# xn^T kn of batches 1 to 7 as seven block products, with its block sums on GpSimd

## The chip, the cores and the metric

The kernel runs on one core of a Trainium2 chip. A core has five engines, each with an instruction queue of its own that it works through in order: TensorE (PE; its weight loads are listed as PEld), VectorE (DVE), ScalarE (ACT), GpSimd (POOL) and SyncE (SP), which here only issues transfers. They meet through semaphores. Matmul results land in PSUM, everything else lives in SBUF. The metric is the time on the device in microseconds (us); less is better.

## The reference, cut to what matters

The input `x` has 8 batches of 1024 rows of 256 channels, in 32-bit floats. The result is `x` plus a linear attention plus a two-layer network, both fed with the normalised `x`.

```python
xn = (x - mean(x)) / sqrt(var(x) + 1e-5)             # per row
q, k, v = split(xn @ qkv_w + qkv_b)                  # 16 heads of 16 channels
q, k = q / max(|q|, 1e-12), k / max(|k|, 1e-12)      # per row and head
kv  = einsum('bhnd,bhne->bhde', k, v)
out = einsum('bhnd,bhde->bhne', q, kv)
ffn = relu(xn @ W1 + b1) @ W2 + b2
return x + out @ proj_w + proj_b + ffn
```

The kernel never forms `v`. It takes G = xn^T kn (256 x 256, kn being the scaled k), multiplies by the weights of v to get the 16 x 16 blocks of `kv`, and folds these with `proj_w` into one 256 x 256 matrix M, so that the attention's output is q M.

## The kernel before

**Tiling.** A batch is 8 tiles of 128 rows. `xn` and `qk` hold rows on partitions; `xnT` and `qT` hold channels on partitions, and come from 32x32 transposes on VectorE (`turn`) whose squares the SP queue moves into place. Batches go in a loop over `b` (line 822) with these steps on PE: `hidden(b)` (the first layer, with small steps put between its products), `project_by_sums(b + 1)` (q and k of the next batch; `project(1)` for batch 1), the first half of `second(b)` (the second layer and q M, up to the `yield` on line 762), `mix_g(b + 1)`, and the second half of `second(b)`.

**Block products.** `hidden`, `project_by_sums` and `second` use a scheme for a product of two 2 x 2 block matrices that takes seven block products for eight. It needs sums of blocks of both factors: four of the left (s1 to s4, `sums_of_a`, line 188) and four of the right (t1 to t4, `sums_of_b`, line 181), some written over a block that is no longer needed (s3, t3). Sums of data are made on GpSimd. Partial results pass from bank to bank as u1, u2, u3 on VectorE.

**The mix.** `mix_g` (line 497) is a plain product: for each of two halves of xn's channels, 8 row tiles, 128 columns of xn as weights against the 256 columns of kn, summed in one bank of the pool `ps_mix`; one ScalarE copy brings the bank to `gT`. It is used by `mix_kv` (line 510) in the next `hidden`. `kn` is there once GpSimd has scaled k in place (line 466, two instructions, at the end of the projection).

**Order.** The program is written in the order wanted (`manual_schedule`), so an engine's queue has its instructions in the order of the Python calls. Within `second`, the banks are a, c_, d, e: products into a and c_, u2 (line 749), a product into d, u3 (line 753), then the function `between` (line 754, `norms_of_q` of the next batch: squares on ScalarE, their sums and inverse roots on VectorE), the product into e, and `join(1, 1)`: an addition of bank, bias and u3 on VectorE (line 719), a transpose on VectorE (line 710), an addition to `xq` on GpSimd (line 715). After that half come the statistics of x of batch b + 2 (`norm_stats`, line 241, `norm_scale`, line 255), the mix, the normalisation (`norm_apply` on ScalarE, line 271), the transposes `turn_x`, the second half of `second`, and `shift`, which adds 1 to the first 128 channels of xn.

**Buffers.** Pool `one` has one buffer per tag, so a tile waits for the last reader of the tile before it under the tag. Pool `psum` hands out seven banks in turn, `ps_mix` is the eighth. Tags that matter: "turn" (the squares of a transpose), "u1" and "u3" (partial results), "xn", "qk", "gT".

Of the kernel before, what the change touches and what calls it, by code (L numbers as in the profile page):

```python
# [9 lines left out]
F32 = mybir.dt.float32  # L10
AF = mybir.ActivationFunctionType
ALU = mybir.AluOpType
# [4 lines left out]
def kernel(  # L17
# [34 lines left out]
    nc = tc.nc  # L52
    P = 128
    B, N, C = x.shape
# [3 lines left out]
    NT = N // P  # L58
    HT = NT // 2
    HN = N // 2  # L60
    KC = C // P
# [10 lines left out]
    big = ctx.enter_context(tc.tile_pool(name="big", bufs=2))  # L72
    one = ctx.enter_context(tc.tile_pool(name="one", bufs=1))
    work = ctx.enter_context(tc.tile_pool(name="work", bufs=2))
    small = ctx.enter_context(tc.tile_pool(name="small", bufs=4))
    psum = ctx.enter_context(tc.tile_pool(name="psum", bufs=7, space=bass.MemoryType.PSUM))
    ps_mix = ctx.enter_context(tc.tile_pool(name="ps_mix", bufs=1, space=bass.MemoryType.PSUM))

# [11 lines left out]
    def bank(shape, name):  # L90

        return psum.tile(shape, F32, tag="bank", name=name)

    xs, xqs, xns, xnTs, xSs, hTs, qks, qTs, mixes, Ms, hSs = ({} for _ in range(11))
# [146 lines left out]
    def norm_stats(b, tiles):  # L241

        xt, n = xs[b], len(tiles)
        st = work.tile([P, NT, 6], F32, tag="st", name=f"st_{b}_{tiles[0]}")[:, :n, :]
        mv = small.tile([P, NT, 2], F32, tag="mv", name=f"mv_{b}_{tiles[0]}")[:, :n, :]
        for i, t in enumerate(tiles):
            nc.vector.bn_stats(st[:, i, :], xt[:, t, :])
        for i in range(n):
            nc.vector.bn_aggr(mv[:, i, :], st[:, i, :])
        rstd = small.tile([P, NT], F32, tag="rstd", name=f"rstd_{b}_{tiles[0]}")[:, :n]  # L250
        nc.scalar.activation(rstd, mv[:, :, 1], AF.Sqrt, bias=eps_sb)
        for i, t in enumerate(tiles):
            stats[b, t] = i, mv, rstd

    def norm_scale(b, tiles, on_act):
        i, mv, rstd = stats[b, tiles[0]]
        nc.vector.reciprocal(rstd, rstd)
        if on_act:
            nmr = small.tile([P, NT], F32, tag="nmr", name=f"nmr_{b}_{i}")[:, : len(tiles)]
            nc.vector.scalar_tensor_tensor(nmr, mv[:, :, 0], -1.0, rstd, ALU.mult, ALU.mult)  # L260
            for t in tiles:
                stats[b, t] += (nmr,)
# [87 lines left out]
    def invert(ss):  # L350

        nc.vector.tensor_scalar_max(ss, ss, L2_EPS * L2_EPS)
        nc.scalar.activation(ss, ss, AF.Sqrt)
        nc.vector.reciprocal(ss, ss)
# [19 lines left out]
    def squares_of(b, n, g, m, ss):  # L374
        sq = work.tile([P, 2, C], F32, tag="yt", name=f"sq_{b}_{n}_{g}_{m}")
        nc.scalar.activation(sq, part_of_qk(b, n, g, m), AF.Square)  # L376
        return lambda: nc.vector.tensor_reduce(
            ss[:, n * HT + 2 * g : n * HT + 2 * g + 2, :],
            sq.rearrange("p w (g d) -> p w g d", d=D), AX.X, ALU.add,
        )  # L380
# [69 lines left out]
    def norms_of_q(b):  # L450
        ss = small.tile([P, NT, H], F32, tag="ssq", name=f"ssq_{b}", bufs=1)
        late = []
        for n in range(2):
            for g in range(2):
                late.append(squares_of(b, n, g, 0, ss))
                if len(late) == 2:
                    late.pop(0)()
        late.pop(0)()
        invert(ss)
        for h in range(2):  # L460
            norms_of[b, h, 0] = ss[:, ts(h, HT), :]
# [9 lines left out]
    def scale_q(b, h):  # L471
        scale(nc.gpsimd if b == 0 else nc.vector, b, h, 0)

    def turn_q(b):

        if b not in qTs:
            qTs[b] = one.tile([P, KC, NP, P, 2], F32, tag="qT", name=f"qT_{b}")
            turns["q", b] = turn(qTs[b], qks[b], f"q_{b}")
        next(turns["q", b])
# [12 lines left out]
    def shift(b):  # L492

        part = xns[b][:, :, 0:P]
        nc.scalar.activation(part, part, AF.Identity, bias=ones)

    def mix_g(b):
        qk, xn = qks[b], xns[b]
        gp = ps_mix.tile([P, KC, C], F32, tag="mix", name=f"gp_{b}")
        for f in range(KC):  # L500
            for t in range(NT):
                nc.tensor.matmul(  # L502
                    gp[:, f, :], xn[:, t, ts(f, P)], qk[:, t, C : 2 * C],
                    start=(t == 0), stop=(t == NT - 1),
                )
        gT = one.tile([P, KC, C], F32, tag="gT", name=f"gT_{b}")
        nc.scalar.copy(gT, gp)
        mixes[b] = gT

    def mix_kv(b):  # L510
        gT = mixes.pop(b)
        kvp = ps_mix.tile([P, KC, P], F32, tag="mix", name=f"kvp_{b}")
        for c in range(KC):
            cols = slice(2 * C + c * P, 2 * C + (c + 1) * P)
            for f in range(KC):
                nc.tensor.matmul(  # L516
                    kvp[:, c, :], wqkv_sb[:, f, cols], gT[:, f, ts(c, P)],
                    start=(f == 0), stop=(f == KC - 1),
                )
        kvm = one.tile([P, KC, P], F32, tag="Mt", name=f"kvm_{b}")  # L520
        for c in range(KC):
            nc.vector.tensor_tensor(
                kvm[:, c, :].rearrange("p (g d) -> p g d", d=D),
                kvp[:, c, :].rearrange("p (g d) -> p g d", d=D),
                blk.unsqueeze(2).to_broadcast([P, G, D]), ALU.mult,
            )
        mixes[b] = kvm
# [126 lines left out]

    def later_steps(b):
        return {
            1: [lambda: mix_kv(b)],
            2: [lambda: scale_q(b, 0)],
            3: [lambda: scale_q(b, 1)],
            4: [lambda: mix_m(b)],  # L660
            5: [lambda: turn_q(b)],
            6: [lambda: turn_q(b)],
            7: [lambda: turn_q(b)],
            8: [lambda: turn_q(b)],

            11: [lambda: sums_of_q(b)],
        }
# [12 lines left out]
                skip_group_check=True,  # L680
            )

    def second(b, between=lambda: None):

        xq, hT, hS, qT, (M, Mt) = xqs[b], hTs[b], hSs[b], qTs[b], Ms[b]
        a11, a12, s3, a22 = (
            [hT[:, i + k * FH, ts(n, HP), :, :] for i in range(FH)] + [qT[:, k, ts(n, HP), :, :]]
            for n in range(2) for k in range(2)
        )
        s1, s2, s4 = ([hS[:, s, i] for i in range(FH + 1)] for s in range(3))  # L690
        b11, t3, b21, b22 = (
            [w2_sb[:, i + k * FH, ts(m, HC)] for i in range(FH)] + [M[:, k, ts(m, HC)]]
            for k in range(2) for m in range(2)
        )
        t1, t2, t4 = ([w2t[:, s, i, :] for i in range(FH)] + [Mt[:, s, :]] for s in range(3))

        def tmp(name):
            pool = work if name in ("u2", "yt") else one
            return pool.tile([P, HP, P, 2], F32, tag=name, name=f"{name}_o_{b}")

        def add(dst, p, q):
            nc.vector.tensor_tensor(dst, p, q, ALU.add)
            return dst
# [37 lines left out]
        a, c_, d, e = (bank([P, HP, P, 2], f"po{s}_{b}") for s in "acde")  # L741
# [4 lines left out]
        u1 = tmp("u1")  # L746
        nc.scalar.copy(u1, a)
        product(c_, t2, s2, True, True)
        u2 = add(tmp("u2"), c_, u1)
        u3 = tmp("u3")  # L750
        for du, u in zip(ds, parts):
            product(du, t3, [r[:, u] for r in s3], True, False)
# [69 lines left out]
    for b in range(B):  # L822
        if b > 0:
            load_squares(b, (0,) if b == B - 1 else (0, 1))
            if b + 2 < B:
                load(b + 2)
        hidden(b)
        if b == 0:
            qTs[0] = one.tile([P, KC, NP, P, 2], F32, tag="qT", name="qT_0")
            turn_on_pe(qTs[0], qks[0], "q_0")  # L830
            sums_of_w2()
            sums_of_q(0)
            shift(1)
        if b + 1 == 1:
            project(1)
            out_parts = second(b)
        elif b + 1 < B:
            project_by_sums(b + 1)
            out_parts = second(b, lambda: norms_of_q(b + 1))
        else:  # L840
            out_parts = second(b)
        next(out_parts)
        if b + 1 == 1:
            sums_of_x(1, 0)
            sums_of_x(1, 1)
            sums_of_wqk()
        if b + 2 < B:
            norm_stats(b + 2, range(NT))
            norm_scale(b + 2, range(NT), True)
        if b + 1 < B:  # L850
            mix_g(b + 1)
        if b + 2 < B:
            norm_apply(b + 2, range(NT))
            for _ in range(R):
                turn_x(b + 2)
        next(out_parts)
        if b + 2 < B:
            shift(b + 2)
# [31 lines left out]
```

## Time and profile before

The time is 623.9 us, the median of three runs (623.89, 623.9 and 624.88). One execution was profiled:

| what | value |
|---|---|
| the profiled execution's time | 624.22 us |
| its span, first to last instruction | 622.1 us |
| granted TensorE clock, share of full speed | 0.997 |
| PE, mix (`gp`, line 502): 256 records, two per matmul | 56.6 us busy, 379 ns each |
| share of the chain that is the mix | 9% |
| PE start to PE start of the mix, each batch from 1 on | 6.9 us |
| GpSimd instructions | 290 |
| idle time of GpSimd before its additions to `xq` (line 715), waiting for the transpose | 181.4 us over 30 |

A profile's "busy" of a matmul counts it to its modelled end, though the next one has begun; how fast PE moves is read from starts. A line of the timeline has the start and the length in us, the engine, the line of the program, the operation, the tiles written and read, the shapes, how many instructions are merged in it, and in brackets how long the engine stood idle before it and what ended that. The chain of waits follows the work that ended last back to the start. In the row of a group, the number after the bar is the busy time, then the mean of one instruction in ns, then idle time before.

### The profile page before, as it was taken

What the parts mean: (1) busy time and instruction counts of PE and PEld (TensorE: products, weight loads), DVE (VectorE), ACT (ScalarE), POOL (GpSimd) and SP (SyncE); (2) the same over time, 40 slices, a digit from 0 to 9 for tenths busy, and PEclk for the clock granted to TensorE, in tenths of its full rate; (3) what the DMA queues carried; (4) which work ended last, traced back from release to release, by engine and by line L of the source; (5) the groups of instructions that cost most, each with busy time, mean ns of one, the idle gap of its engine ahead of it and who ended that gap; (6) DMA issues with size and microseconds to landing.
All of it is one profiled execution on the core that took longest, in us unless ns stands there. A gap on an engine that the chain in (4) does not pass through costs nothing.

```text
span 622.1 us, 6098 instructions
## 1 busy us (share of the span) xinstructions
PE 612.8 (98%) x1843; PEld 344.2 (55%) x1843; DVE 398.8 (64%) x698; ACT 209.0 (34%) x348; POOL 351.1 (56%) x290
## 2 busy tenths in 40 slices
PE   8999999999999999999999999999999999999996
PEld 5465455556644666447564484644755557545454
DVE  6776735777648766577456874667845677428823
ACT  4356304352143422343242532325224352003500
POOL 3568927399315991269902797029951399414701
PEclk9999999999999999999999999999999999999998
DMA  7734001490025700285004820058101470004202
GB/s 232 141 59 136 1 0 29 112 188 11 0 51 127 161 1 1 68 156 116 0 1 101 189 49 0 6 129 178 29 0 26 112 132 2 0 3 99 67 0 67
DMA packets 139503, 43.26 MB, mean 70 GB/s; under 512 B 135880, under 2 KB 136272, under 8 KB 139472
## 3 DMA queue, kind: packets, MB, share of 16 engines
q1 hardware_dynamic: 139472, 42.89, 31.1%
q8 instruction: 14, 0.23, 0.2%
q14 instruction: 17, 0.14, 0.1%
HBM read 19.80 MB, written 8.39 MB: 45 GB/s over the span
## 4 chain that ended last, share of the span: by engine, by line
PE 96%; DVE 2%; DMA 1%; ACT 0%; issue 0%; SPq 0%; DVEq 0%; ACTq 0%
PE poe L678 11%; PE poa L678 11%; PE pod L678 10%; PE gp L502 9%; PE pha L555 8%; PE phe L555 8%; PE phd L555 8%; PE poc L678 6%; PE pq L330 5%; PE phc L555 4%; PE pqe L398 3%; PE pqa L398 3%; PE pqd L398 3%; PE pqc L398 2%; PE kvp L516 1%; PE mp L533 1%
## 5 line engine op out<-in xcount | busy, mean ns | idle before, releaser
L715 POOL TENSOR_TENSOR xq<-xq,yt_o 128x512 f32<-128x512 f32 x30 | 37.9, 1262 | 181.4 <-DVE yt_o L710 181.4
L562 ACT ACTIVATE hT<-hT,b_sb 128x512 f32<-128x512 f32 x96 | 68.8, 722 | 63.4 <-DVE hT L567 58.8
L190 POOL TENSOR_TENSOR hS<-hT 128x512 f32<-128x512 f32 x31 | 45.8, 1478 | 56.4 <-issue 41.5
L376 ACT ACTIVATE sq<-qk 128x512 f32<-128x512 f32 x48 | 29.0, 629 | 109.3 <-DVE qk L404 59.1
L555 PE MATMUL pha<-xnT,w_sb 128*128 128x512 f32 x128 | 65.4, 592 | 0.0
L678 PE MATMUL poa<-hT,w_sb 128*128 128x512 f32 x128 | 57.5, 592 | 0.0
L502 PE MATMUL gp<-qk,xn 128*128 128x256 f32 x256 | 56.6, 379 | 0.0
L502 PEld LDWEIGHTS gp<-qk,xn 128*128 128x128 f32 x256 | 48.6, 190 | 9.6 <-issue 3.3
L567 DVE TENSOR_TENSOR hT<-phe,u 128x512 f32<-128x512 f32 x64 | 43.7, 683 | 6.6 <-PE phe L555 4.9
L710 DVE STREAM_TRANSPOSE yt_o<-y_o 128x512 f32<-128x512 f32 x30 | 33.0, 1099 | 16.2 <-ACT y_o L765 13.9
L192 POOL TENSOR_TENSOR hS<-hT,hS 128x512 f32<-128x512 f32 x31 | 39.5, 1275 | 2.4
L191 POOL TENSOR_TENSOR hS<-hS,hT 128x512 f32<-128x512 f32 x31 | 39.4, 1272 | 2.4
L194 POOL TENSOR_TENSOR hT<-hT 128x512 f32<-128x512 f32 x31 | 40.0, 1290 | 0.0
L678 PEld LDWEIGHTS poa<-hT,w_sb 128*128 128x128 f32 x128 | 24.3, 190 | 25.0 <-issue 24.2
L297 DVE STREAM_TRANSPOSE turn_x<-xn 128x512 f32<-128x512 f32 x28 | 17.7, 685 | 31.1 <-ACT xn L271 31.1
L555 PEld LDWEIGHTS pha<-xnT,w_sb 128*128 128x128 f32 x128 | 23.8, 190 | 23.4 <-issue 20.8
L567 DVE TENSOR_TENSOR u<-phc,u 128x512 f32<-128x512 f32 x32 | 21.8, 681 | 20.0 <-ACT u L581 10.6
L581 ACT COPY u<-pha 128x512 f32<-128x512 f32 x32 | 18.4, 574 | 43.9 <-PE pha L555 43.9
L562 ACT ACTIVATE hT<-pha,b_sb 128x512 f32<-128x512 f32 x32 | 21.8, 682 | 33.1 <-PE pha L555 33.1
L555 PE MATMUL phe<-xS,w1t 128*128 128x512 f32 x64 | 32.7, 592 | 0.0
L555 PE MATMUL phd<-xnT,w_sb 128*128 128x512 f32 x64 | 32.7, 592 | 0.0
L555 PE MATMUL phc<-xS,w1t 128*128 128x512 f32 x64 | 32.7, 592 | 0.0
(165 smaller groups left out, 1189.6 us busy)
## 6 DMA issues: line engine op xcount, KB each, us to landing
xq<-in_L_attn_x_dram SPq DMA_DIRECT2D x60, 128.0 KB, 3.8
out_dram<-xq SPq DMA_DIRECT2D x60, 128.0 KB, 2.9
x<-in_L_attn_x_dram SPq DMA_DIRECT2D x14, 512.0 KB, 5.8
xnT<-turn_x SPq DMA_DIRECT2D x112, 64.0 KB, 2.1
qT<-turn_q SPq DMA_DIRECT2D x112, 64.0 KB, 2.2
x<-in_L_attn_x_dram SPq DMA_DIRECT2D x4, 256.0 KB, 4.0
w_sb<-in_L_ffn_W_dram SPq DMA_DIRECT2D x2, 512.0 KB, 7.0
w_sb<-in_L_ffn_W_dram SPq DMA_DIRECT2D x8, 128.0 KB, 3.1
```

Of the source, the lines that this page charges most:

```text
L190: eng.tensor_tensor(s1, a21, a22, ALU.add)
L191: eng.tensor_tensor(s2, s1, a11, ALU.subtract)
L192: eng.tensor_tensor(s4, a12, s2, ALU.subtract)
L194: eng.tensor_tensor(a21, a11, a21, ALU.subtract)
L398: nc.tensor.matmul(dst[:, w, :], a[:, g, :, w], rhs, start=start and w == 0, stop=stop, skip_group_check=True,)
L502: nc.tensor.matmul(gp[:, f, :], xn[:, t, ts(f, P)], qk[:, t, C : 2 * C], start=(t == 0), stop=(t == NT - 1),)
L555: nc.tensor.matmul(dst, lhsT, rhs, start=start, stop=stop, skip_group_check=True)
L562: nc.scalar.activation(block(i, n, m), src, AF.Relu, bias=b1_sb[:, fc : fc + 1])
L567: nc.vector.tensor_tensor(dst, p, q, ALU.add)
L678: nc.tensor.matmul(dst, l, r, start=start and n == 0, stop=stop and n == len(lhs) - 1, skip_group_check=True,)
L710: nc.vector.transpose(yt.rearrange("p u w r c -> p u r w c"), y.rearrange("p u (s r) w -> p u r w s", r=R),)
L715: nc.gpsimd.tensor_tensor(xh, xh, yt.rearrange("p u w r c -> p (u w) r c"), ALU.add)
```

## The change

For batches 1 to 7 the mix is made by the seven-product scheme, with the two row halves of the batch as the inner blocks and the two channel halves as the outer ones; batch 0 keeps `mix_g`. Each product has 128 x 128 weights and 128 moving columns, over four row tiles. It uses the bank of `ps_mix` and three of `psum`; five additions on VectorE and two copies on ScalarE join them into `gT`. The eight block sums are all on GpSimd: s3 and s2 of batch b + 1 in `hidden(b)` (part 0; for batch 1 just before part 1), t1, s1, t2 and t3 after the projection (part 1), t4 and s4 at the place of `between` (part 2). s3 goes over a block of xn and t3 over a block of kn; s1, s4, t1 and t2 take the buffer "turn", t4 takes "u1", s2 a new one, and the partial results of the mix take "u3". The statistics of x of batch b + 2 move from behind the first half of `second` to a place between u2 and u3. Pool `small` goes from four buffers to two.

```diff
-    small = ctx.enter_context(tc.tile_pool(name="small", bufs=4))
+    small = ctx.enter_context(tc.tile_pool(name="small", bufs=2))
...
+    gsums = {}
+    def blocks_of_xn(b):
+        return [xns[b][:, ts(n, HT), ts(f, P)] for f in range(KC) for n in range(2)]
+    def blocks_of_kn(b):
+        return [
+            qks[b][:, ts(n, HT), C + f * P : C + (f + 1) * P] for n in range(2) for f in range(KC)
+        ]
+    def g_sums(b, part):
+        a11, a12, a21, a22 = blocks_of_xn(b)
+        b11, b12, b21, b22 = blocks_of_kn(b) if part else [None] * 4
+        def tile_of(tag, name):
+            return one.tile([P, HT, P], F32, tag=tag, name=f"g{name}_{b}")
+        def sub(dst, p, q, op=ALU.subtract):
+            nc.gpsimd.tensor_tensor(dst, p, q, op)
+        if part == 0:
+            s2 = tile_of("gs2", "s2")
+            sub(a21, a11, a21)
+            sub(s2, a22, a21)
+            gsums[b] = [s2]
+        elif part == 1:
+            gs = one.tile([P, 4, HT, P], F32, tag="turn", name=f"gs_{b}")
+            s1, s4, t1, t2 = (gs[:, i] for i in range(4))
+            sub(t1, b12, b11)
+            sub(s1, gsums[b][0], a11, ALU.add)
+            sub(t2, b22, t1)
+            sub(b12, b22, b12)
+            gsums[b] += [s1, s4, t1, t2]
+        else:
+            s2, s1, s4, t1, t2 = gsums[b]
+            t4 = tile_of("u1", "t4")
+            sub(t4, b21, t2)
+            sub(s4, a12, s2)
+            gsums[b] = [s1, s2, s4, t1, t2, t4]
+    def mix_g_by_sums(b):
+        a11, a12, s3, a22 = blocks_of_xn(b)
+        b11, t3, b21, b22 = blocks_of_kn(b)
+        s1, s2, s4, t1, t2, t4 = gsums.pop(b)
+        a = ps_mix.tile([P, P], F32, tag="mix", name=f"gpa_{b}")
+        c_, d, e = (bank([P, P], f"gp{s}_{b}") for s in "cde")
+        us = one.tile([P, 3, P], F32, tag="u3", name=f"u_g_{b}")
+        def mm(dst, l, r, start, stop):
+            for t in range(HT):
+                nc.tensor.matmul(
+                    dst, l[:, t, :], r[:, t, :], start=start and t == 0,
+                    stop=stop and t == HT - 1, skip_group_check=True,
+                )
+        def add(dst, p, q):
+            nc.vector.tensor_tensor(dst, p, q, ALU.add)
+        mm(a, a11, b11, True, False)
+        nc.scalar.copy(us[:, 0], a)
+        mm(e, s1, t1, True, False)
+        mm(c_, s2, t2, True, True)
+        add(us[:, 1], c_, us[:, 0])
+        mm(d, s3, t3, True, False)
+        add(us[:, 2], d, us[:, 1])
+        gT = one.tile([P, KC, C], F32, tag="gT", name=f"gT_{b}")
+        add(gT[:, 1, P:C], e, us[:, 2])
+        mm(a, a12, b21, False, True)
+        nc.scalar.copy(gT[:, 0, 0:P], a)
+        mm(d, a22, t4, False, True)
+        add(gT[:, 1, 0:P], d, us[:, 1])
+        mm(e, s4, b22, False, True)
+        add(gT[:, 0, P:C], e, us[:, 1])
+        mixes[b] = gT
...
+            0: [lambda: g_sums(b + 1, 0)] if b + 1 < B else [],
...
-    def second(b, between=lambda: None):
+    def second(b, early=lambda: None, between=lambda: None):
...
         u2 = add(tmp("u2"), c_, u1)
+        early()
...
             project(1)
-            out_parts = second(b)
         elif b + 1 < B:
             project_by_sums(b + 1)
-            out_parts = second(b, lambda: norms_of_q(b + 1))
+        if b + 1 < B:
+            if b == 0:
+                g_sums(1, 0)
+            g_sums(b + 1, 1)
+            def early():
+                if b + 2 < B:
+                    norm_stats(b + 2, range(NT))
+                    norm_scale(b + 2, range(NT), True)
+            def between():
+                g_sums(b + 1, 2)
+                if b > 0:
+                    norms_of_q(b + 1)
+            out_parts = second(b, early, between)
         else:
...
-        if b + 2 < B:
-            norm_stats(b + 2, range(NT))
-            norm_scale(b + 2, range(NT), True)
         if b + 1 < B:
-            mix_g(b + 1)
+            mix_g_by_sums(b + 1)
```

## The prediction, made before the changed kernel ran

> **What bounds the kernel.** I read the page first: busy shares, then the chain that ended last.
>
> ```profile
> PE 612.8 (98%) x1843; PEld 344.2 (55%) x1843; DVE 398.8 (64%) x698; ACT 209.0 (34%) x348; POOL 351.1 (56%) x290
> ...
> PE 96%; DVE 2%; DMA 1%; ACT 0%; issue 0%; SPq 0%; DVEq 0%; ACTq 0%
> ```
>
> TensorE (PE) is busy for 98% of the span, and 96% of the chain is its own work. So time falls only if PE has less to do and does not wait for what replaces it. Next I read PE's timeline in the stage of batch 3, where `mix_g(4)` runs; the five middle stages differ from it by at most 0.3 us.
>
> ```profile
> 313.95 1.02 PE L678 MATMUL poe<-hS,Mt 128*128 128x512 f32 x2
> 314.81 7.07 PE L502 MATMUL gp<-qk,xn 128*128 128x256 f32 x32
> 321.72 3.60 PE L678 MATMUL poa<-hT,w_sb 128*128 128x512 f32 x8
> ...
> 338.02 1.05 PE L516 MATMUL kvp<-gT,wqkv_sb 128*128 128x128 f32 x8
> 338.92 1.02 PE L555 MATMUL pha<-xnT,w_sb 128*128 128x512 f32 x2
> ```
>
> Take the starts: the mix holds PE from 314.81 to 321.72, 6.91 us for 32 records (a float matmul leaves two), 0.216 us each. The 128-column `kvp` takes from 338.02 to 338.92 for 8 records, 0.112 us each. Nothing stands idle between groups.
>
> **What PE gains.** Seven products x 4 row tiles x 2 records = 56 records of the `kvp` form, 128 x 128 weights and 128 moving columns. 56 x 0.112 = 6.27 us against 6.91: 0.64 us less per batch, 4.5 us over batches 1 to 7. Batch 0 keeps the old mix.
>
> A rule of the Trainium skill speaks against this (TensorE: Matmul & The Clock Gate, Back-to-back issue gap): in a stream of weight load and matmul pairs a 128-column matmul was measured at about 81 ns and a 512-column one at about 131, so narrow ones cost far more per column. A straight line gives 98 at 256 columns, so halving the width would save 17%: an estimate of 0.216 x 0.83 = 0.179 us a record, 10.0 us a batch, 3.1 us MORE, and 21.8 us more in all. The row halves almost exactly (0.112 to 0.216), is of this data type and alternates weights as the products will, so I take the row. It shows only eight records in a row, hence a small chance for the page.
>
> **GpSimd (POOL).** Eight subtractions or additions of 128x512 are added per batch. The row, and the queue around the mix:
>
> ```profile
> L191 POOL TENSOR_TENSOR hS<-hS,hT 128x512 f32<-128x512 f32 x31 | 39.4, 1272 | 2.4
> ```
>
> ```profile
> 306.08 3.83 POOL L466 TENSOR_TENSOR qk<-qk,ssk 128x1024 f32<-128x1024 f32 x2
> 317.49 1.26 POOL L715 TENSOR_TENSOR xq<-xq,yt_o 128x512 f32<-128x512 f32 x1 [7.58 <-DVE yt_o L710]
> ...
> 336.83 1.26 POOL L715 TENSOR_TENSOR xq<-xq,yt_o 128x512 f32<-128x512 f32 x1 [3.02 <-DVE yt_o L710]
> 345.01 2.21 POOL L190 TENSOR_TENSOR hS<-hT 128x512 f32<-128x512 f32 x1 [6.92 <-issue]
> ```
>
> Part 0 (two operations, 2.6 us) comes behind the add of 336.83, in the 6.92 us before 345.01: nothing, if it ends before the first sum of the hidden values is due. Its input is long there. Parts 1 and 2 follow the scaling of k, which ends at 309.91. Successive POOL operations start 1.23 us apart (1.35 where one needs the last), so t1 runs from 309.87, s1 311.10, t2 312.33, t3 313.56, t4 314.80, s4 316.03 to 317.30. With mix start 314.81, the products want: second (s1, t1) 315.71; third (t2) 316.60; fourth (t3) 317.50; sixth (t4) 319.28; seventh (s4) 320.18. Every sum is 2.7 us or more early. The `xq` add behind them needs its transpose from VectorE anyway. In batch 0 all eight start at 80.9 and end by 91.2; the first `xq` add was at 92.58. Cost: 0.
>
> The operand strides are new. The nearest rows give 1.26 us (strided `xq`) and 1.27; the scaling with broadcast takes 1.94 for 1,024, so 0.97 per 512; the worst row is 2.21. I take 1.27, and keep 0.97 and 2.21 for the range.
>
> **VectorE (DVE)** is where it is tight.
>
> ```profile
> 306.50 0.69 DVE L702 TENSOR_TENSOR u_o<-poc,u_o 128x512 f32<-128x512 f32 x1 [3.84 <-PE poc L678]
> 310.72 0.69 DVE L702 TENSOR_TENSOR u_o<-pod,u_o 128x512 f32<-128x512 f32 x1 [3.53 <-PE pod L678]
> ...
> 314.07 0.23 DVE L352 TENSOR_SCALAR ssq<-ssq 128x128 f32<-128x128 f32 x1
> 314.68 0.95 DVE L354 RECIPROCAL ssq<-ssq 128x128 f32<-128x128 f32 x1 [0.38 <-ACT ssq L353]
> 315.55 0.65 DVE L719 SCALAR_TENSOR_TENSOR y_o<-poe,ob,u_o 128x512 f32<-128x512 f32 x1
> 316.30 1.11 DVE L710 STREAM_TRANSPOSE yt_o<-y_o 128x512 f32<-128x512 f32 x1
> 317.34 2.67 DVE L247 BATCH_NORM_STATS2 st<-x 128x6 f32<-128x256 f32 x8
> ...
> 321.15 0.17 DVE L260 SCALAR_TENSOR_TENSOR nmr<-mv,rstd 128x8 f32<-128x8 f32 x1
> ```
>
> The statistics last from 317.34 to 321.32, 3.98 us. They move from behind the first join into the 3.53 us gap before 310.72: from 307.10 to about 311.1. What they pass on DVE is u3, the q norms, the join (L719) and its transpose; on ScalarE their square root comes ahead of the four q squares, two of which ran at 302.62 and now run at about 310.7, in time for their reductions. They issue no DMA, and pass nothing on SP or POOL. So u3 is 0.45 us late, and so is all that follows it.
>
> Then a lock:
>
> ```profile
> L352 DVE TENSOR_SCALAR ssk<-ssk x6: 976/988/1098, 150.7 to 524.8; 128x128 f32<-128x128 f32 x6
> L352 DVE TENSOR_SCALAR ssq<-ssq x6: 226/227/228, 164.4 to 538.5; 128x128 f32<-128x128 f32 x6
> ```
>
> The same small operation takes 0.23 us where POOL is idle (q) and 0.99 where POOL computes (k), ending about 0.08 us after the POOL operation. SBUF — State Buffer, Who interferes with whom, has the rule: VectorE's two-port forms and operations with two SBUF inputs share ports with POOL, and the second to issue blocks until the first finishes. POOL used to be idle at 314.07. Now the q operation comes at 314.52, under t3 (to 314.83), and should end at 314.91, 0.38 us long. The row taken flat would say 0.99, ending at 315.51; by the rule what counts is which POOL operation it meets. I take 0.38. The tiny L260 is caught likewise, for 0.1 us, counted in the 0.45. By the same rule the join is free, with one SBUF tensor beside PSUM; L567, of that kind, took 0.68 us under a busy POOL.
>
> From there, by the old spacings: reciprocal 315.28, join 316.15, transpose 316.91, first new add 318.0. The new adds are like the row `kvm<-kvp,blk`, 128x128 out of PSUM, 0.28 us: u1+c to 318.3; u2 waits for the fourth product (end 318.55) and lasts to 318.84; the e add to 319.2. PE wants u2 for the sixth product's weights at 319.16 and the e add for the seventh at 320.07. So 0.3 us is left, and the cost is 0. Were this cover gone, each 0.1 us of lateness would be 0.1 us of PE. The two adds behind the last products are followed by x's transposes, which wait for ScalarE anyway.
>
> **ScalarE** gets two copies of 128x128 for one of 128x512 (0.58 us). No such PSUM copy is in the trace: above 0, at most 0.58; nearest is the 128x128 root at 0.31, taken. The first reuses the buffer u3, so it waits for the join to have read it: 316.85 to 317.2, before the add at 318.0 and the fifth product at 318.39. The last matmul that reads xn ends before the mix does, so the normalisation starts sooner than before. Cost 0.
>
> **Banks, buffers.** Three more of the seven banks per stage: the third bank of the next hidden pass is now the one that the last join (L719, ending 0.95 us after its product) empties, while PE wants it 1.72 us after: 0. Fewer `small` buffers: a statistic is replaced two batches on: 0.
>
> **Sum.** 7 x 0.64 = 4.5 us off the profiled execution's 624.22 (span 622.1, to 617.6) is 619.7. The median is 623.9, so 619.4; the seams of seven short groups get 0.1. Forecast **619.5**.
>
> **Rivals.**
> - *The lock takes the gain.* If the q operation comes 0.3 us later, or t3 ends 0.3 earlier, it meets t4 and ends at 316.15: join 317.4, u2 at 319.9, sixth product 319.95 instead of 319.28. That is 0.67 us in each of five stages, all their gain; the stages of batches 0 (no q norms) and 6 (no statistics) keep theirs. 623.9 - 1.3 = 622.6. For: the margin is 0.3 us, and the stage of batch 2 already runs 0.28 late. Against: four of five stages repeat to 0.01 us. One to four stages caught give 620.1 to 622.
> - *POOL sums late (slower).* At the row's 2.21 us each the last sum ends at 309.87 + 13.3 = 323.1 and the mix at 324.0, against 321.72: +2.3 us in all seven stages, 640.0. It breaks even where s4 ends at 320.8, from 1.83 us an operation. Against: 2.21 is a POOL operation that itself sat behind a two-input VectorE one (L466), and none runs here.
> - *Narrow matmuls at the page's price:* 623.9 + 21.8 = 645.7.
> - *PE doesn't wait but nothing is saved* (records at 0.123 us, weight loads as the limit): 623.9. Against: loads keep 0.112 in `kvp`.
>
> **Chances.** Forecast 0.70 (own range 618.3 to 620.4: records of 0.109, as in transposes, give 0.9 to 1.2 less; 0.1 us of stall a stage gives 0.7 more). Lock 0.17, most of it in part. POOL late 0.05, page's price 0.03, no saving 0.05. A difference under 0.2%, 1.25 us, can't be told from none. Faster takes the forecast and most of the lock: 0.83; same 0.09; slower 0.08. Range for 8 in 10: 618.2 to 622.6, from the narrow records to the lock in all five stages.
>
> **What would show it.** PE: seven groups of 8 records in about 6.3 us, with no idle time before the sixth. POOL: six operations of 1.27 us back to back, the last ending 2.5 us after the mix starts; two more in the old 6.92 us gap. DVE: L352 for q at 0.3 to 0.5 us; near 1.0 is the lock. Wrong if PE idles before a mix product for over 0.2 us a stage, if records take over 0.115 us, or if the first hidden sum on POOL starts late.

## The result, and the profile after

The changed kernel takes **619.38 us** (median of 4 runs, 619.09 to 620.73); the kernel before takes 624.12 in the runs beside it. The ratio is 0.9926, with a 95% interval of 0.9909 to 0.9943: faster by 4.7 us. The prediction was 619.5.

From the page of the changed kernel, the busy shares and the chain of waits:

```profile
PE 609.8 (99%) x2011; PEld 346.1 (56%) x2011; DVE 409.6 (66%) x733; ACT 210.1 (34%) x355; POOL 421.0 (68%) x346
...
PE 96%; DVE 2%; DMA 1%; issue 0%; ACT 0%; SPq 0%; DVEq 0%; ACTq 0%
```

GpSimd has 70 us more work, VectorE 11, and PE is still the chain. PE's timeline in the same stage as in the prediction, that of batch 3 (start, length, engine, line, operation):

```profile
313.43 1.02 PE L759 MATMUL poe<-hS,Mt 128*128 128x512 f32 x2
314.29 1.05 PE L565 MATMUL gpa<-qk,xn 128*128 128x128 f32 x8
315.18 1.06 PE L565 MATMUL gpe<-gs 128*128 128x128 f32 x8
316.07 1.06 PE L565 MATMUL gpc<-gs,gs 128*128 128x128 f32 x8
316.97 1.06 PE L565 MATMUL gpd<-qk,xn 128*128 128x128 f32 x8
317.86 1.06 PE L565 MATMUL gpa<-qk,xn 128*128 128x128 f32 x8
318.75 1.06 PE L565 MATMUL gpd<-gt,xn 128*128 128x128 f32 x8
319.65 1.06 PE L565 MATMUL gpe<-qk,gs 128*128 128x128 f32 x8
320.54 1.88 PE L759 MATMUL poa<-hT,w_sb 128*128 128x512 f32 x4
```

Seven groups start 0.89 us apart, none has idle time in brackets, and the mix (from its first start to that of the next `poa`) takes 320.54 - 314.29 = 6.25 us where it took 6.91. GpSimd, same stage:

```profile
309.36 1.27 POOL L532 TENSOR_TENSOR gs<-qk 128x512 f32<-128x512 f32 x1
310.59 1.27 POOL L532 TENSOR_TENSOR gs<-gs,xn 128x512 f32<-128x512 f32 x1
311.82 1.27 POOL L532 TENSOR_TENSOR gs<-qk,gs 128x512 f32<-128x512 f32 x1
313.05 1.26 POOL L532 TENSOR_TENSOR qk<-qk 128x512 f32<-128x512 f32 x1
314.28 1.26 POOL L532 TENSOR_TENSOR gt<-qk,gs 128x512 f32<-128x512 f32 x1
315.51 1.27 POOL L532 TENSOR_TENSOR gs<-xn,gs 128x512 f32<-128x512 f32 x1
...
338.23 1.27 POOL L532 TENSOR_TENSOR gs<-xn 128x512 f32<-128x512 f32 x1
343.78 2.26 POOL L190 TENSOR_TENSOR hS<-hT 128x512 f32<-128x512 f32 x1 [4.28 <-ACT hT L642]
```

The first six lines are the six sums of parts 1 and 2, back to back. Part 0 for the next batch ends at 339.50, in a gap of which 4.28 us are still idle, and what ends the idle time is ScalarE's input for the next sum. VectorE:

```profile
313.92 0.48 DVE L352 TENSOR_SCALAR ssq<-ssq 128x128 f32<-128x128 f32 x1
314.78 0.95 DVE L354 RECIPROCAL ssq<-ssq 128x128 f32<-128x128 f32 x1 [0.38 <-ACT ssq L353]
315.65 0.65 DVE L800 SCALAR_TENSOR_TENSOR y_o<-poe,ob,u_o 128x512 f32<-128x512 f32 x1
316.40 1.11 DVE L791 STREAM_TRANSPOSE yt_o<-y_o 128x512 f32<-128x512 f32 x1
317.44 0.25 DVE L571 TENSOR_TENSOR u_g<-gpc,u_g 128x128 f32<-128x128 f32 x1
318.06 0.29 DVE L571 TENSOR_TENSOR u_g<-gpd,u_g 128x128 f32<-128x128 f32 x1 [0.37 <-PE gpd L565]
```

The join is line 800 and its transpose line 791. Behind the transpose comes the mix's first addition, and then VectorE waits 0.37 us for PE's fourth product: it is early, not late. Line 352 is the floor under the squared norms of q. It takes 0.48 us instead of 0.23: the lock of the prediction is there, with t3 (313.05 to 314.31), and the floor ends 0.09 us after t3.

The profiled execution took 620.73 us, the longest of the four: PE had half its clock for one stretch of 3.4 us near the start (the granted clock is 0.59 from 8 to 12 us, where that of the kernel before is 1.00), and its first mix began at 35.75 us instead of 34.43. From mix start to mix start the middle stages have gone from 74.82 us to 74.17.

### The profile page after: what moved, and what is told of

Its sections match the earlier page's. It is cut to its first block, busy times and chain, and to the rows that moved or that the text cites. A ratio compares the mean times of both kernels' runs of the same rounds, so it can differ in the third digit from the quotient of the medians.

```text
span 619.0 us, 6600 instructions
## 1 busy us (share of the span) xinstructions
PE 609.8 (99%) x2011; PEld 346.1 (56%) x2011; DVE 409.6 (66%) x733; ACT 210.1 (34%) x355; POOL 421.0 (68%) x346
## 4 chain that ended last, share of the span: by engine, by line
PE 96%; DVE 2%; DMA 1%; issue 0%; ACT 0%; SPq 0%; DVEq 0%; ACTq 0%
PE poa L759 11%; PE poe L759 11%; PE pod L759 10%; PE pha L635 8%; PE phe L635 8%; PE phd L635 8%; PE poc L759 6%; PE pq L330 5%; PE phc L635 4%; PE pqa L398 3%; PE pqe L398 3%; PE pqd L398 3%; PE gpe L565 2%; PE gpd L565 2%; PE gpa L565 2%; PE pqc L398 2%
## 5 line engine op out<-in xcount | busy, mean ns | idle before, releaser
L635 PE MATMUL phe<-xS,w_sb 128*128 128x512 f32 x64 | 32.7, 592 | 0.0
L635 PE MATMUL phd<-xnT,w1t 128*128 128x512 f32 x64 | 32.7, 592 | 0.0
L271 ACT ACTIVATE xn<-x,nmr,rstd 128x256 f32<-128x256 f32 x56 | 28.4, 587 | 6.6 <-PE gpd L565 4.1
```

What stands on the lines that cost most here:

```text
L635: nc.tensor.matmul(dst, lhsT, rhs, start=start, stop=stop, skip_group_check=True)
```

## Experiments

A time in the expectations that counts from the mix is from PE's start of its first product. All edits are to the changed kernel; all measured times are medians.

**1. The statistics back behind the join.**

```diff
             def early():
-                if b + 2 < B:
-                    norm_stats(b + 2, range(NT))
-                    norm_scale(b + 2, range(NT), True)
+                pass
...
+        if b + 2 < B:
+            norm_stats(b + 2, range(NT))
+            norm_scale(b + 2, range(NT), True)
         if b + 1 < B:
             mix_g_by_sums(b + 1)
```

> The changed kernel, but with the statistics of x of batch b+2 back behind the join, ahead of the mix's additions on VectorE. Theory (the additions are on PE's path and the move keeps VectorE free for them): the join now comes 1.4 us after the mix starts, its transpose ends at 3.2, the statistics at 7.1, u2 at 7.8, so the sixth product starts at 7.9 instead of 4.5: 3.4 us lost in each of five stages and 2.4 in that of batch 0, 19 us in all, 638. Rival (VectorE has room and the place of the statistics is of no account): 619.4.

Measured: 649.26 us, ratio 1.0398 (1.038 to 1.0416), slower than either figure expected. PE and ScalarE around the mix in the stage of batch 3:

```profile
330.34 1.06 PE L565 MATMUL gpd<-qk,xn 128*128 128x128 f32 x8
334.54 1.47 PE L565 MATMUL gpa<-qk,xn 128*128 128x128 f32 x8 [3.14 <-ACT u_g L574]
335.80 1.91 PE L565 MATMUL gpd<-gt,xn 128*128 128x128 f32 x8
337.50 1.61 PE L565 MATMUL gpe<-qk,gs 128*128 128x128 f32 x8
338.95 1.45 PE L759 MATMUL poa<-hT,w_sb 128*128 128x512 f32 x3
```

```profile
334.03 0.30 ACT L251 ACTIVATE rstd<-mv,eps_sb 128x8 f32<-128x8 f32 x1 [5.94 <-DVE mv L249]
334.24 0.25 ACT L574 COPY u_g<-gpa 128x128 f32<-128x128 f32 x1
```

Two things were not in the expectation. First, PE stops at the fifth product, not the sixth: it adds to bank a, which ScalarE has to copy first, and the copy (line 574) stands in ScalarE's queue behind the square root of the statistics (line 251), which waits for VectorE. Second, after the stop the records run slower: in the view by stretches (length; busy time of PE, PEld, DVE, ACT, POOL; granted clock),

```profile
327.60:339.00 11.40, 8.26 (x58) 8.01 (x57) 7.37 (x26) 2.23 (x7) 3.78 (x4) 0.85 0.01 1
339.00:347.00 8.00, 8.00 (x20) 3.56 (x20) 3.78 (x6) 4.67 (x8) 1.26 (x1) 1.00 0.17 40
```

the clock is 0.85 over the mix and 1.00 behind it, as it was before it. From the starts, the wait costs 334.54 - 330.34 - 0.89 = 3.31 us, and the three products behind it 338.95 - 334.54 = 4.41 instead of 2.68, 1.73 more. Over the six stages the mixes took 10.25, 11.22, 12.16, 11.29, 11.27 and 12.15 us: 30.8 more than six times 6.25, of which the waits are about 19, the size expected, and the clock the other 12. VectorE's second addition ended 7.7 us after the mix's start, as expected (7.8), so by this estimate its path alone would have held the sixth product about as long as the copy held the fifth. The theory stands in that the place of the statistics costs PE. The expectation lacked the copy on ScalarE, and its cost was too low by what the clock took.

**2. All sums and the moved statistics, with the old product.**

```diff
         if b + 1 < B:
-            mix_g_by_sums(b + 1)
+            gsums.pop(b + 1)
+            mix_g(b + 1)
```

> The changed kernel with all eight sums on GpSimd and the moved statistics, but with the old product of 32 records for the mix (what it multiplies is then partly sums, so the output is not the reference's; the work is of the same size). Theory (all of the gain is the shorter mix; sums and move cost nothing beside it): mix 6.9 us plus at most 0.1 of wait for t3, 623.9 to 624.6. Rival (the move of the statistics or earlier buffers bring part of the gain): 619.5 to 622.5. Rival (the sums cost time elsewhere): over 625.

Measured: 624.89 us, ratio 1.0016 (1.0006 to 1.0026).

```profile
314.15 1.02 PE L759 MATMUL poe<-hS,Mt 128*128 128x512 f32 x2
315.07 7.17 PE L502 MATMUL gp<-qk,xn 128*128 128x256 f32 x32
322.08 0.59 PE L759 MATMUL poa<-hT,w_sb 128*128 128x512 f32 x1
```

The mix starts 0.92 us after `poe` where two such records take 0.86, and holds PE for 7.01 us: 0.16 in all. Its first matmuls here read t3, which ends at 315.02, 0.05 us before they start. In six stages that is 1.0 us, and the kernel is 0.8 slower than before. So 70 us of new work on GpSimd, and a move of 4 us of VectorE work in six stages, show nowhere else. The gain is the shorter product.

**3. Part 0 not a stage ahead.**

```diff
-            0: [lambda: g_sums(b + 1, 0)] if b + 1 < B else [],
...
-            if b == 0:
-                g_sums(1, 0)
+            g_sums(b + 1, 0)
             g_sums(b + 1, 1)
```

> The changed kernel with part 0 (s3, s2) not a stage ahead but in front of part 1 in every stage, so that eight sums follow the scaling of k. Theory (a slack of 2.5 us on GpSimd): t3 ends 2.65 us after the mix starts where its weights are wanted at 2.57, all other sums are in time: 0.1 us lost in six stages, 619.4 to 620.2. Rival (the sums are on the path, so two more of them show in full): 2.5 us in each of six stages, 634.

Measured: 619.51 us, ratio 0.9926 (0.9912 to 0.9941). The mixes took 6.29 to 6.32 us in the six stages, that of batch 0 6.25. The fourth and the fifth product:

```profile
315.23 1.12 PE L565 MATMUL gpd<-qk,xn 128*128 128x128 f32 x8
316.19 1.06 PE L565 MATMUL gpa<-qk,xn 128*128 128x128 f32 x8
```

They start 0.96 us apart instead of 0.89: the fourth product waits some 0.06 us for t3. The two sums made a stage ahead are worth 0.3 us over the kernel, less than a run shows. GpSimd's slack of 2.5 us is as worked out: two sums just fit.

**4. Three more sums on GpSimd ahead of t1.**

```diff
             s1, s4, t1, t2 = (gs[:, i] for i in range(4))
+            for _ in range(3):
+                sub(s4, a22, a11)
             sub(t1, b12, b11)
```

> The changed kernel with three more sums of the same size on GpSimd ahead of t1 (into s4, which is written over later). Theory (slack of 2.5 us, then every microsecond counts): s1 ends 1.25 us after the mix starts, t2 2.5, t3 3.7, s4 6.2; the mix takes 7.35 us instead of 6.25 in six stages, that of batch 0 has 0.9 us more slack and loses nothing: 626. Rival (GpSimd has far more room): 619.4. Rival (no slack): 3 x 1.23 us in six stages, 641.

Measured: 627.55 us, ratio 1.0052 (1.0035 to 1.0068); mixes of 7.7 us in six stages, 6.25 in that of batch 0.

```profile
240.04 1.05 PE L567 MATMUL gpa<-qk,xn 128*128 128x128 f32 x8
241.61 1.16 PE L567 MATMUL gpe<-gs 128*128 128x128 f32 x8 [0.52 <-POOL gs L532]
242.84 1.16 PE L567 MATMUL gpc<-gs,gs 128*128 128x128 f32 x8
244.07 1.16 PE L567 MATMUL gpd<-qk,xn 128*128 128x128 f32 x8
```

The second, third and fourth product start 1.23 us apart, GpSimd's pace, instead of 0.89. The loss is 1.45 us a stage, not 1.1: the three extra sums write the same tile and start 1.35 us apart instead of 1.23, which makes s1 0.27 us later than I had it. The remaining 0.1 is what PE needs to start again after a wait (the fifth product starts 0.99 us after the fourth instead of 0.89).

**5 and 6. VectorE 0.6 us later, with and without the locked operation.**

```diff
             def between():
                 g_sums(b + 1, 2)
+                if 0 < b and b + 2 < B:
+                    more = work.tile([P, NT, 6], F32, tag="st", name=f"more_{b}")
+                    for i in range(2):
+                        nc.vector.bn_stats(more[:, i, :], xs[b + 2][:, i, :])
```

> The changed kernel with two more row statistics (0.33 us apart) on VectorE between u3 and the q norms, in the stages of batches 1 to 5. Theory (the lock): the floor under the squared norms of q (line 352) comes 0.27 us after the mix starts instead of 0.38 before, misses the end of t3 and waits for the end of t4 at 1.25: it takes about 1.0 us, the join starts at 2.6, u2 ends at 5.1, the sixth product starts 0.65 us late in five stages: 622.6. Rival (no lock, the 0.49 us of the profile have another cause and stay): the chain is 0.65 late, u2 ends at 4.7, 0.3 us lost in five stages: 621. Rival (the floor would take its 0.23 us of an idle GpSimd): no loss, 619.4.

and, on top of it, in `norms_of_q`:

```diff
-        invert(ss)
+        nc.scalar.activation(ss, ss, AF.Sqrt)
+        nc.vector.reciprocal(ss, ss)
```

> The kernel of e5_dve_late without the floor (1e-24) under the squared norms of q, in the stages from batch 1 on: the one VectorE operation of this chain that shares GpSimd's ports is left out, the two more statistics stay. Theory (the lock is what costs time in e5): join at 1.5, u2 not later than the fourth product allows, no loss: 619.4. Rival (VectorE's work itself is what is too much): the two statistics still show, 621.

Measured: 622.72 us (ratio 0.9978, 0.9971 to 0.9984) with the floor, 619.13 (0.9921, 0.9904 to 0.9937) without it. VectorE, GpSimd, ScalarE and PE of the first:

```profile
314.31 1.06 DVE L352 TENSOR_SCALAR ssq<-ssq 128x128 f32<-128x128 f32 x1
...
316.61 0.65 DVE L800 SCALAR_TENSOR_TENSOR y_o<-poe,ob,u_o 128x512 f32<-128x512 f32 x1
...
318.75 0.29 DVE L571 TENSOR_TENSOR u_g<-gpd,u_g 128x128 f32<-128x128 f32 x1
```

```profile
314.01 1.27 POOL L532 TENSOR_TENSOR gt<-qk,gs 128x512 f32<-128x512 f32 x1
```

```profile
317.35 0.27 ACT L574 COPY u_g<-gpa 128x128 f32<-128x128 f32 x1 [1.64 <-DVE y_o L800]
```

```profile
317.67 1.16 PE L565 MATMUL gpa<-qk,xn 128*128 128x128 f32 x8
319.19 1.13 PE L565 MATMUL gpd<-gt,xn 128*128 128x128 f32 x8 [0.36 <-DVE u_g L571]
```

The mix began at 314.07, and the times that follow count from there. The floor came at 0.24, behind the end of t3, and took 1.06 us, to the end of t4 (314.01 to 315.28). In the changed kernel it came 0.37 us before the mix's start and was through at 0.11; here it came 0.61 us later and was through 1.19 later, at 1.30. The sixth product started at 5.12 instead of 4.46, and the five mixes took 6.97 to 7.00 us instead of 6.25. A second path is used up at the same point: ScalarE's copy takes the buffer that the join reads, so it waits for the join, ends at 3.55, and the fifth product starts at 3.60 instead of 3.57, with 0.1 us more between its first records.

Without the floor the same two extra operations cost nothing: all mixes 6.25. But that run takes about 0.5 us of work out of VectorE's chain along with the lock (first addition 3.24 us after the mix's start, 3.15 in the changed kernel), so it doesn't say which of the two mattered. Hence run 8.

**8. As late as in run 5, with an operation of the same size that doesn't wait for GpSimd.** To run 5's kernel, in `norms_of_q`:

```diff
-        invert(ss)
+        nc.vector.tensor_reduce(ss, ss.unsqueeze(3), AX.X, ALU.add)
+        nc.scalar.activation(ss, ss, AF.Sqrt)
+        nc.vector.reciprocal(ss, ss)
```

> The kernel of run 5 (the roots, the floor of q and the scale of q come ahead of the additions in VectorE's program), with one operation exchanged: in place of the floor of q (a tensor_scalar, which kept GpSimd waiting for the shared lock in run 5) stands a tensor_reduce of the same size that adds over an axis of length 1, so it copies its input; from batch 1 on the floor of 1e-24 under q's squared norms is left out. Theory (what costs in run 5 is that the floor holds the lock while GpSimd adds t3, so that t3 and all behind it come late; VectorE itself may start its first addition some 0.3 to 0.5 us later): t3 is added as in the changed kernel, the second addition ends about 4.2 us after the mix starts, TensorE asks for it at 4.35: no loss, 619.4. Rival (it is VectorE's lateness itself that costs, lock or no lock): 0.65 us in each of five stages again, 622.7.

Measured: 620.41 us, ratio 0.9938 (0.9921 to 0.9954). The profiled execution took 619.07, and its mixes 6.25 to 6.27 us. VectorE, GpSimd and PE in the stage of batch 3, whose mix began at 312.59:

```profile
312.85 0.29 DVE L459 TENSOR_REDUCE ssq<-ssq 128x128 f32<-128x128 f32 x1
...
316.18 0.25 DVE L573 TENSOR_TENSOR u_g<-gpc,u_g 128x128 f32<-128x128 f32 x1
316.53 0.29 DVE L573 TENSOR_TENSOR u_g<-gpd,u_g 128x128 f32<-128x128 f32 x1
```

```profile
312.57 1.27 POOL L534 TENSOR_TENSOR gt<-qk,gs 128x512 f32<-128x512 f32 x1
```

```profile
317.06 1.06 PE L567 MATMUL gpd<-gt,xn 128*128 128x128 f32 x8
```

The exchanged operation came at 0.26, as the floor did in run 5 (0.24), under the same sum t4, and took 0.29 us instead of 1.06. The second addition ended 4.23 us after the mix's start (4.06 in the changed kernel, 4.97 in run 5), and PE did not wait. The sixth product started at 4.47 (4.46 in the changed kernel). So the theory stands in its main point: of the 1.19 us by which run 5's chain was late, 0.44 come from the extra work and are free, and 0.75 are the lock's. These cost PE 0.74 us in each of five stages (0.66 up to the start of the sixth product, the rest in its slower start). Five times 0.74 is 3.7 us, by which the two profiled executions differ (622.78 and 619.07).

The wording of the expectation had the lock's victim wrong: counted from the mix, the sums on GpSimd start where they did, within 0.06 us, in all four kernels (the changed one and runs 5, 6 and 8); it is VectorE that waits.

By the medians the exchange brings back 2.3 us. Run 8's lies 1.0 us above the changed kernel's, because the other three executions took 620.40 to 620.47; there is no trace of these, and their 1.3 us more is not explained (their spans are 1.3 longer too). A difference of that size arises ahead of the first mix: it begins at 35.75 and 36.08 us in the two profiled executions with a stretch of half clock near the start (the changed kernel and run 7), and at 33.86 to 34.43 in the other eight. Whether the three had such a stretch is not known.

**7. t4 and s4 on VectorE.**

```diff
             def between():
-                g_sums(b + 1, 2)
                 if b > 0:
...
-            sub(t4, b21, t2)
-            sub(s4, a12, s2)
+            nc.vector.tensor_tensor(t4, b21, t2, ALU.subtract)
+            nc.vector.tensor_tensor(s4, a12, s2, ALU.subtract)
...
+            g_sums(b + 1, 2)
             mix_g_by_sums(b + 1)
```

> The changed kernel with part 2 (t4, s4) on VectorE, behind the join and ahead of the mix's additions; GpSimd ends with t3. Theory (it is the free engine that counts, not the fast one): the join's transpose ends 3.2 us after the mix starts, t4 and s4 take 0.69 us each behind it, u2 ends at 5.0 and the sixth product starts 0.7 us late in the six stages from batch 1 on (that of batch 0 has 1 us of room): 623.7. If GpSimd's addition to xq gets in between them, as both read two tensors in SBUF, s4 waits for it, u2 ends at 6.4 and 2.1 us are lost in each of the six stages: 632. Rival (VectorE does such an operation in 0.69 us and GpSimd in 1.27, so the sums are better there): 619.4 or less.

Measured: 630.08 us, ratio 1.009 (1.0073 to 1.0107); mixes of 8.0 us in six stages and 6.95 in that of batch 0.

```profile
322.01 0.65 DVE L550 TENSOR_TENSOR gt<-qk,gs 128x512 f32<-128x512 f32 x1
322.58 1.75 DVE L551 TENSOR_TENSOR gs<-xn,gs 128x512 f32<-128x512 f32 x1
...
322.17 1.62 POOL L796 TENSOR_TENSOR xq<-xq,yt_o 128x512 f32<-128x512 f32 x1 [3.27 <-DVE yt_o L791]
```

(The first two lines are VectorE's timeline, the last GpSimd's, of the stage of batch 3.) GpSimd's addition was issued under t4 and took 1.62 us instead of 1.26; s4 was then issued under the addition and took 1.75 us where t4 had taken 0.65, ending 0.54 after the addition. It is the second of the two cases expected. I had it at 632: the loss was 1.75 us a stage instead of 2.1, but batch 0's stage, expected to lose nothing, lost 0.7.

## Why the prediction was right

| step | predicted | measured |
|---|---|---|
| a 128-column record | 0.112 us | 0.112 |
| mix | 6.27 us, no wait | 6.25, no wait |
| a sum on GpSimd | 1.27 us | 1.26 to 1.28 |
| last sum (s4), end after mix start | 2.5 us | 2.5 |
| floor of q | 0.38 us long, ends 0.10 after mix start | 0.48 to 0.49, ends 0.11 |
| join, start after mix start | 1.34 us | 1.35 to 1.36 |
| u2, end after mix start | 4.03 us | 4.06 |
| a 128x128 addition; copy | 0.28; 0.31 us | 0.29; 0.27 |

**What bounds it.** PE did, and does. Run 2 takes the shorter product away and leaves all else: the gain is gone.

**The narrow product.** The 0.112 us of the row held over 56 records in a row. Of the Trainium skill's warning (TensorE: Matmul & The Clock Gate, Back-to-back issue gap) that narrow matmuls cost far more per column, nothing is seen in this kernel: half the columns took 0.52 of the time (0.112 against 0.216 us). By the prediction's estimate from its figures the kernel would have taken 645.7.

**GpSimd.** Nothing to pay, with a slack that runs 3 and 4 put at two sums and under three. The strided operands take what contiguous ones do.

**VectorE and the lock.** The chain came out within 0.03 us, as its parts kept the spacings that they had. The floor was called 0.1 us too short because it starts 0.08 us sooner than I had it; it ends with t3 all the same, so the error went no further. In the stage of batch 6, where no statistics are ahead of it, it starts 0.73 us before the mix and takes 0.86: it too ends with t3, and the join comes at 1.37 there, at 1.35 to 1.36 in the others. The stage of batch 2, which ran 0.28 us late before, now runs like the others (its floor 0.38 us before the mix). The room was 0.25 us at the second addition: in run 5 it ended 0.91 us later than in the changed kernel and the sixth product started 0.66 later. Run 8 used 0.17 of it and lost nothing. The rival of the lock had its place, its mechanism and nearly its price right: 0.67 us a stage called, 0.66 measured up to the sixth product and 0.74 by the mix's end. The changed kernel just doesn't reach the point from which it decides: its floor came 0.39 us ahead of the end of t3, and in run 5, 0.61 us later, it came behind that end.

**Moved statistics.** Their place is what makes the scheme pay: run 1 shows 30 us between the two places, 12 of them through the clock. The prediction moved them off VectorE's path to the mix; that the root on ScalarE would hold PE as well was in neither the prediction nor run 1's expectation.

**Banks and buffers.** No time is lost behind the mix: the stage shortened by 0.65 us, the mix by 0.66. The banks and the fewer buffers were not tried apart.

**The luck in it.** The terms in the table were right to 0.1 us or better. That the total fell within 0.12 us of the forecast is partly luck: the four executions spread over 1.6 us (619.09 to 620.73), and the kernel before moved by 0.2 between its two medians.

## What to carry to other kernels

When one engine is the whole chain, price a rewrite by its start-to-start pace on that engine at the new shape, from the nearest row of the same type. Then give every new input a time at which it is wanted and one at which it is there; the smallest difference is the risk, and here it was 0.25 us. A slow engine with slack beats a fast one that is on the path (run 7), and when GpSimd is made busy, look for the short VectorE operations that wait for it: the floor took 0.23 us alone and 0.48 to 1.06 here, until the GpSimd operation that it met had ended. Where an operation is moved past others, look at every engine on which it issues something: the 0.30 us root on ScalarE held PE in run 1.

## What the runs showed of the hardware that was not expected

- A stop of PE of 2.1 us (batch 0's stage in run 1, by the modelled ends) was followed by records at half speed, with 1.7 us lost. So were the five stops of 3.14 us, with 1.7 us lost in three mixes and 2.6 in two (there the clock stayed low past the mix, for 0.4 us more). Stops of 0.36 us (run 5), 0.5 (run 4) and 1.5 (run 7, six times) left the granted clock at 1.00. The length of the stop does not decide alone: near the start, half clock also followed stops of 1.03 us (the changed kernel) and 0.84 (run 7), where the kernel before had a stop of 1.00 and kept its clock. What else decides is open.
- After a wait, the first two records of a product start 0.18 to 0.21 us apart instead of 0.11 (run 5, fifth and sixth product), so a wait costs up to 0.1 us more than its length. The sixth product's first weight load started 0.03 us before its record there, where in the changed kernel it runs 0.11 ahead; that this is the cause is argued, not shown.
